# z of two images projected during the first scan, PE's pieces admitted by their weight, and DVE's readers of PE placed behind the product

## The chip, the core and the metric

The kernel runs on one core of a Trainium2 chip. A core has five engines, each of which takes its own instructions in order: PE (TensorE, matrix products and transposes into PSUM), DVE (VectorE), ACT (ScalarE), POOL (GpSimd) and SP (SyncE, which here issues nearly all DMAs). [...] The metric is the device time of one execution in microseconds (us); lower is better.

## What is computed

Four images of 384 channels and 48 x 48 pixels go through four layers, each of the form x + layer(group norm(x)). Cut to what matters here:

```
# layer 0, a selective scan over the 2304 pixels (D_INNER 768, D_STATE 16)
xz = xs @ in_proj_w.T;  xin, z = split(xz)            # z is what is moved
xin = silu(causal_conv4(xin) + conv_b)
dt, B, C = split(xin @ x_proj_w.T);  dt = softplus(dt @ dt_proj_w.T + dt_proj_b)
h[t] = exp(dt*A) * h[t-1] + dt*B[t]*x[t]              # per channel and state
y[t] = sum_s h[t]*C[t] + xin*D
out = layer_norm((y * silu(z)) @ out_proj_w.T)
# layer 1: 1x1 conv, 8x8 FFT filter, 3x3 depthwise conv, gelu gate, 1x1 conv
# layer 2: 11x11 depthwise conv with kernels built from 4 points
# layer 3: 4 experts (384 -> 384 -> 384), the two best of them weighted by a router
```

z depends on the input image alone: it needs the group norm's mean and deviation of x, and x. Nothing of the recurrence enters it.

## The kernel before

**Chunks and scans.** Layer 0 is worked in chunks of 460 (the last 464) pixels, five an image, twenty in all (`G`). A chunk has 96 scans, one for a block of 128 channels (6 blocks, taken in pairs) and one of 16 states. A scan is one DVE instruction over the 460 pixels. The main loop in `scans` (line 556 on) has one turn, or slot, for each of the 1920 scans; within it every engine's instructions are written out by hand in the order in which they are to stand (`tc.manual_schedule`).

In slot u: ACT makes the decay `da` a few scans ahead (L826), POOL makes the drive `bu` three scans ahead (L837), DVE scans (L850), and the state is multiplied with C, in "fast" slots by DVE at once (`product_now`, L870), in "slow" slots by POOL in the next slot (`product`, L879). A third of the slots are slow in image 0, a half afterwards. PE transposes each product and adds it into y (`turned`, L770). B and C arrive by DMA, spread over the partitions (`spread`, L814), some slots ahead.

**Everything else is tasks.** Each other part of the work is a generator that yields before every step the kind of step ("pe", "act", "dve", "pool"), a weight, the PSUM ring it needs room in, and a condition. A `Lane` (L92) holds a queue and a few active tasks. In each slot the lanes are asked twice: for ACT steps at the start, and after the scan for all others; each task makes at most one step per call. `wait(n)` is n empty steps.

There are three lanes. `aux` holds the rest of layer 0, planned by `plan` (L984) with a due slot for each task in a chunk: `project` (x of the next chunk), `project_z` (z of this one, L666 to L684), `gates` (silu), `expand`, `steps`, `gate` (y times z, L895), `out_proj`, `layer_norm`, `residual`, and for the next image `image_stats`, `image_norm` and `fold`, which scales a half of in_proj's weights by the image's deviation. `one` holds layers 1 to 3's router of the image before (`later`, L1127), `two` the experts of that image (`experts`, L1547). So image 0's scan has only `aux` beside it, the next three scans run beside the later layers of the image before, and after the last scan come what is left of the experts of image 2, and image 3's layers 1 to 3.

**The backlog.** `Meter` (L62) keeps an estimate of PE's backlog in us. Each slot drains 2.3 and adds 0.44 for the scan's transposes; a step of PE adds its weight. A lane other than `aux` may not start a weighted step while the value is over the limit:

```
if weight and self.bound and self.meter.value > self.meter.limit:
    continue
...
meter = Meter(2.3, 2.0)
```

**What DVE does between scan and product.** Steps of kind "dve" of all lanes stand after `scan(u)` and before `product_now(u)`. Many of them read a result of PE out of PSUM: an expert's output (`ye` L1641, `xe` L1644), layer 1's and 2's results (`uf` L1225, `xr` L1311, `xb` L1437), the gate (`zs` L907) and the experts' bias (`nb` L1587).

## Time and profile before

| | us |
|---|---|
| median of 3 runs | 5437.34 |
| lowest, highest | 5428.49, 5438.78 |
| the profiled execution | 5425.31 |
| its span, first to last instruction | 5423.4 |

The profile's page gives for the whole span PE 86% busy, DVE 75%, POOL 62%, ACT 55%. Those are averages over stages with different limits. The span in 40 slices of 136 us shows them (digits are tenths of busy time):

```profile
PE   5677677687678988988789999988899999999899
DVE  5999989889998788899887778899977674452200
POOL 3878878876678788765667678775777673000000
PEclk8788788788789999999899999999999999999899
```

Slices 1 to 7 are image 0's scan, up to slice 33 follow the other three, and the rest is the tail. A row of the windows, which the prediction uses, gives for a stretch "from:to length", then for each engine its busy time and, in brackets, its instructions; then PE's granted clock as a share of full speed, the mean busy share of the 16 DMA engines, and GB/s. A matmul of 32-bit numbers is two records. Busy times of PE are unions of overlapping records, so the mean length of one matmul in the groups is longer than what it costs in a row of many.

The products of z alone, by the windows restricted to their tile, for the scans of images 0, 1, 2 and 3 (PE, PE's weight loads, ACT, then clock and DMA of the stretch):

```profile
87.00:1016.50 929.50, 85.12 (x180) 36.01 (x180) 19.11 (x30) 0.81 0.47 136
1016.50:2128.30 1111.80, 81.22 (x180) 35.43 (x180) 19.01 (x30) 0.87 0.49 141
2128.30:3338.00 1209.70, 74.56 (x180) 31.70 (x180) 19.18 (x30) 0.95 0.56 162
3338.00:4525.00 1187.00, 75.91 (x180) 32.40 (x180) 19.14 (x30) 0.95 0.57 160
```

### The profile page before, as it was taken

To read this page: it belongs to the slowest core of one execution; us is meant where nothing else is said; L and a number is where in the kernel's file an instruction comes from. 1 tells how busy PE (TensorE), PEld (TensorE's weight loads), DVE (VectorE), ACT (ScalarE), POOL (GpSimd) and SP (SyncE) were. 2 spreads that over 40 slices of the span, in tenths; PEclk is the share of its full clock that TensorE was granted. 3 is DMA by queue.
4 is the path that set the end of the run, shared out by engine and by line. 5 is a ranking of instruction groups with operands and counts; after the bars stand their busy time and mean duration, and the time that the engine had idled before them with its cause. 6 is when DMAs were issued, how large, how long until landed. Compare 5 with 4: busy or idle time off the path is not lost. (4 is left out here: it accounts for less than half of the span.)

```text
span 5423.4 us, 81753 instructions
## 1 busy us (share of the span) xinstructions
PE 4666.9 (86%) x27796; PEld 3676.0 (68%) x27796; DVE 4053.8 (75%) x5581; ACT 2985.2 (55%) x6632; POOL 3365.2 (62%) x3020
## 2 busy tenths in 40 slices
PE   5677677687678988988789999988899999999899
PEld 4444454454347767665678887765678878889799
DVE  5999989889998788899887778899977674452200
ACT  3565565565558765655467655665566653334321
POOL 3878878876678788765667678775777673000000
PEclk8788788788789999999899999999999999999899
DMA  4445445454345555644566566554655554543200
GB/s 123 138 136 148 127 128 146 126 150 132 106 129 150 146 161 164 177 143 139 155 169 176 149 170 171 156 158 129 170 157 169 157 167 143 166 140 112 64 27 23
DMA packets 628391, 758.95 MB, mean 140 GB/s; under 512 B 58869, under 2 KB 622181, under 8 KB 627582
## 3 DMA queue, kind: packets, MB, share of 16 engines
q1 hardware_dynamic: 617668, 751.98, 48.2%
q8 instruction: 221, 3.62, 0.3%
q10 hardware_dynamic: 10298, 1.67, 0.2%
q14 instruction: 204, 1.67, 0.1%
HBM read 663.81 MB, written 89.65 MB: 139 GB/s over the span
## 5 line engine op out<-in xcount | busy, mean ns | idle before, releaser
L837 POOL TENSOR_TENSOR bu<-u,B 128x460 f32<-128x460 f32 (+1 forms) x1920 | 2227.5, 1170 | 778.2 <-DVE g L850 395.5
L826 ACT ACTIVATE da<-dt,a_neg 128x460 f32<-128x460 f32 (+1 forms) x1920 | 1242.8, 649 | 281.9 <-DVE g L870 185.4
L770 PE MATMUL y<-ident,g 128*115 128x128 f32 (+1 forms) x7680 | 1140.2, 297 | 274.1 <-DVE g L870 164.1
L770 PEld LDWEIGHTS y<-ident,g 128*115 128x115 f32 (+1 forms) x7680 | 1011.0, 187 | 502.3 <-DVE g L870 199.2
L879 POOL TENSOR_TENSOR g<-g,C 128x460 f32<-128x460 f32 (+1 forms) x885 | 1030.5, 1164 | 276.8 <-ACT carry L864 270.4
L850 DVE TENSOR_TENSOR_SCAN da<-da,carry,bu 128x460 f32<-128x460 f32 (+1 forms) x828 | 971.3, 1173 | 133.3 <-ACT da L826 94.7
L850 DVE TENSOR_TENSOR_SCAN g<-da,carry,bu 128x460 f32<-128x460 f32 (+1 forms) x708 | 819.7, 1167 | 83.5 <-ACT da L826 35.3
L870 DVE TENSOR_TENSOR g<-da,C 128x460 f32<-128x460 f32 (+1 forms) x1035 | 653.9, 632 | 91.7 <-PE y L770 31.5
L864 ACT COPY carry<-da 128x1 f32<-128x1 f32 x828 | 130.5, 158 | 824.3 <-DVE g L870 821.2
L1609 PE MATMUL pout<-hr,we 128*128 128x144 f32 x3456 | 483.6, 296 | 41.7 <-ACT hr L1625 31.7
L1609 PEld LDWEIGHTS pout<-hr,we 128*128 128x128 f32 x3456 | 455.4, 196 | 64.9 <-ACT hr L1625 42.6
L1609 PE MATMUL ph<-xe,we 128*128 128x144 f32 x3456 | 470.1, 291 | 13.4 <-DMA xe<-x3d 7.5
L1609 PEld LDWEIGHTS ph<-xe,we 128*128 128x128 f32 x3456 | 446.8, 194 | 30.6 <-issue 7.6
L1416 PE MATMUL pc<-band,row 128*128 128x162 f32 (+14 forms) x3456 | 458.8, 287 | 6.3 <-ACT row L1403 6.0
L1416 PEld LDWEIGHTS pc<-band,row 128*128 128x128 f32 x3456 | 446.2, 196 | 11.9 <-ACT row L1403 7.5
L1274 DVE SCALAR_TENSOR_TENSOR dw<-pad,w_dw,dw 128x384 f32<-128x384 f32 x576 | 347.6, 614 | 17.6 <-ACT pad L1249 6.7
L642 PE MATMUL pin<-xch,w_inx 128*128 128x463 f32 (+2 forms) x720 | 327.9, 595 | 34.7 <-DMA xch<-in_x 15.2
L921 PE MATMUL po<-w_out,zs 128*115 128x384 f32 (+1 forms) x960 | 341.5, 499 | 6.9 <-DVE dt L750 6.4
L1625 ACT ACTIVATE hr<-ph,nb 128x144 f32<-128x144 f32 x576 | 176.4, 377 | 305.2 <-PE ph L1609 303.6
L674 PE MATMUL pinz<-xch,w_inz 128*128 128x460 f32 (+1 forms) x720 | 316.8, 578 | 0.0
L1383 ACT ACTIVATE rep<-x,br,wr 128x192 f32<-128x192 f32 x576 | 274.3, 541 | 4.2 <-issue 4.2
L661 DVE SCALAR_TENSOR_TENSOR xc<-pin,conv_w,xc 128x460 f32<-128x460 f32 (+1 forms) x360 | 249.2, 692 | 30.9 <-ACT xc L655 19.2
(202 smaller groups left out, 5797.6 us busy)
## 6 DMA issues: line engine op xcount, KB each, us to landing
B<-bcd SPq DMA_DIRECT2D x768, 230.0 KB, 3.5
C<-bcd SPq DMA_DIRECT2D x768, 230.0 KB, 3.7
B<-bcd SPq DMA_DIRECT2D x192, 232.0 KB, 3.7
C<-bcd SPq DMA_DIRECT2D x192, 232.0 KB, 4.2
xe<-x3d SPq DMA_DIRECT2D x192, 216.0 KB, 2.8
ye<-y3d SPq DMA_DIRECT2D x144, 216.0 KB, 2.8
y3d<-ye SPq DMA_DIRECT2D x96, 216.0 KB, 2.2
xs<-x1d SPq DMA_DIRECT2D x24, 576.0 KB, 4.6
```

The source lines that it names most:

```text
L642: nc.tensor.matmul(ps[:, lo : halo + n], lhsT=w_inx[:, k, bass.ts(j, P)], rhs=c["x"][:, k, lo : halo + n], start=k == 0, stop=k == CT - 1,)
L674: nc.tensor.matmul(ps[:, :n], lhsT=w_inz[:, k, bass.ts(j, P)], rhs=c["x"][:, k, DCONV - 1 : DCONV - 1 + n], start=k == 0, stop=k == CT - 1,)
L770: nc.tensor.matmul(c["y", m][:w, bass.ts(k, P)], lhsT=src[:, bass.ts(k, w)], rhs=ident, is_transpose=True, start=c["terms", m] == 1 and k ...
L826: nc.scalar.activation(da[:, :n], c["dt", p][:, m % 2, :n], AF.Exp, scale=a_neg[:, m, s : s + 1])
L837: nc.gpsimd.tensor_mul(bu[:, :n], c["u", p][:, m % 2, :n], live["B", u // 2][:, :n])
L850: nc.vector.tensor_tensor_scan(here[:, :n], da[:, :n], bu[:, :n], last if t else nil[:, 0:1], ALU.mult, ALU.add,)
L870: nc.vector.tensor_mul(live["g", u][:, :n], live["h", u][:, :n], live["C", u // 2][:, :n])
L879: nc.gpsimd.tensor_mul(g[:, :n], g[:, :n], live["C", u // 2][:, :n])
L921: nc.tensor.matmul(ps[:w, :C], lhsT=c["zs"][:, m, bass.ts(k, w)], rhs=w_out0[:, m, :], start=m == 0, stop=m == MT - 1,)
L1274: nc.vector.scalar_tensor_tensor(v, src, w_dw[:, ct, k : k + 1], v, ALU.mult, ALU.add)
L1416: nc.tensor.matmul(d["acc2"][0][:, : BANDS[k] * W].rearrange("p (h w) -> p h w", w=W)[:, lo - edges[k] : hi - edges[k], xlo:xhi], lhsT=d[" ...
L1609: nc.tensor.matmul(ps[:, bass.ts(m, EB)], lhsT=w[:, k, bass.ts(m, P)], rhs=of[:, k, :], start=k == 0, stop=k == CT - 1,)
```

## The change

Three things are changed together.

*z of images 3 and 2 early.* A new lane `start` (width 4, bound by the meter) runs in image 0's scan, between `aux` and the other lanes. For images 3 and 2 it takes the statistics of x, normalises, folds z's half of in_proj, loads x chunk by chunk, makes z and stores it to DRAM (`zd`). In the scans of images 2 and 3 `project_z` fetches the chunk's z with one DMA into `zs`, and the statistics of x and the fold of z fall away there.

*The backlog.* The weight of the step itself counts, and the limit is 3.7 in place of 2.0.

*A third call of the lanes in each slot.* Kind "late" stands behind `product_now`. Steps of DVE that read a PSUM result of `gate`, `patches` (`uf`), `finish_strip` (`xr`), `windows` (`xb`), the experts' `begin` (`nb`) and `block` (`ye`, `xe`) become "late"; other DVE steps, also those that read PSUM in `project`, `steps` or `residual`, stay where they were. A task makes no two steps in one slot, whatever their kinds.

```diff
+PHASE = {"act": 0, "late": 2}
...
     def move(self, slot=0):
-        self.after = slot + 1 if self.next and self.next[0] == "act" else 0
+        self.after = slot + 1 if self.next else 0
...
-    def step(self, act, slot, at=0):
+    def step(self, phase, slot, at=0):
...
-            if (kind == "act") != act or task.after > slot:
+            if PHASE.get(kind, 1) != phase or task.after > slot:
                 continue
-            if weight and self.bound and self.meter.value > self.meter.limit:
+            if weight and self.bound and self.meter.value + weight > self.meter.limit:
                 continue
...
+            def early_stats(b, ct, h):
+                yield ("pool", 0, (early["xs"], 1))
+                t, k = early["xs"].take(f"xs0_{b}_{ct}_{h}")
+                half = HW // 2
+                nc.sync.dma_start(t, a["x"][b, bass.ts(ct, P), bass.ts(h, half)])
+                yield from wait(4)
+                st = early["stats", b]
+                for k3 in range(3):
+                    yield ("dve",)
+                    nc.vector.bn_stats(st[:, ct, h, k3, :], t[:, bass.ts(k3, LB)])
+                early["xs"].done(k)
...
+            def early_fold(b):
...
+                nc.sync.dma_start(w, per_channel(a["L0_in_proj_wT"])[:, :, DI:])
+                yield from wait(4)
+                for k in range(CT):
+                    yield ("act",)
+                    nc.scalar.activation(
+                        w[:, k, :], w[:, k, :], AF.Copy, scale=rstd0[:, b, k : k + 1]
+                    )
+                yield ("pe", 2.0, (ring, 1))
+                ps, r = ring.take(f"pbz{b}")
...
+            def early_load(b, t):
+                yield ("pool", 0, (early["x"], 1))
+                x, _ = early["x", b, t] = early["x"].take(f"xz{b}_{t}")
+                cols = bass.ds(starts[t], CHUNKS[t])
+                nc.sync.dma_start(x[:, :, : CHUNKS[t]], strip(a["x"][b], cols))
+                yield from wait(4)
+
+            def early_z(b, t, j):
+                n = CHUNKS[t]
+                x, xk = early["x", b, t]
+                yield ("pe", 2.3, (ring, 1), lambda: early["z"].free())
+                ps, r = ring.take(f"pz{b}_{t}_{j}")
+                z, zk = early["z"].take(f"z{b}_{t}_{j}")
+                for k in range(CT):
+                    nc.tensor.matmul(
+                        ps[:, :n],
+                        lhsT=early["w", b][:, k, bass.ts(j, P)],
+                        rhs=x[:, k, :n],
+                        start=k == 0,
+                        stop=k == CT - 1,
+                    )
...
+                yield ("act",)
+                nc.scalar.activation(
+                    z[:, :n], ps[:, :n], AF.Identity, bias=early["nz", b][:, j : j + 1]
+                )
+                ring.done(r)
+                yield ("pool",)
+                nc.sync.dma_start(zd[b][bass.ts(j, P), bass.ds(starts[t], n)], z[:, :n])
+                early["z"].done(zk)
...
             def project_z(i, j):
                 (b, t), c = G[i], st[i]
                 n, d = CHUNKS[t], batch[b]
+                if b in EARLY:
+                    if j == 0:
+                        c["zs"] = wk.tile([P, MT, TM], F32, name=f"zs{b}_{t}", tag="zs", bufs=1)
+                        nc.sync.dma_start(
+                            c["zs"][:, :, :n],
+                            zd[b].rearrange("(m p) t -> p m t", p=P)[:, :, bass.ds(starts[t], n)],
+                        )
+                    yield from wait(5)
+                    return
                 yield ("pe", 2.3, (ring, 1))
...
-                yield ("dve",)
+                yield ("late",)
                 zm = c["zs"][:, m, :n]
                 nc.vector.tensor_tensor(zm, ps[:, :n], zm, ALU.mult)
...
+            EARLY = (3, 2)
+            zd = {b: dram.tile([DI, HW], F32, name=f"zd{b}") for b in EARLY}
...
+            start = Lane(4, meter)
+            start.queue += early_tasks()
...
                 for u in range(N + 6):
+                    if u == LEN * NC:
+                        start.drain(u)
+                        first_image.close()
...
-                    for lane in (aux, *lanes):
-                        lane.step(False, u)
+                    for lane in (aux, start, *lanes):
+                        lane.step(1, u)
                     if u < N:
                         product_now(u)
+                    for lane in (aux, start, *lanes):
+                        lane.step(2, u)
...
-        meter = Meter(2.3, 2.0)
+        meter = Meter(2.3, 3.7)
```

## The prediction

> **What bounds the kernel now.** Three views, read in this order. First the windows of the run by stage: preparation, the scans of images 0, 1, 2 and 3 (cut where scan 0, 480, 960, 1440 starts), and the tail behind the last scan.
>
> ```profile
> core 0: us, PE busy (x) PEld busy (x) DVE busy (x) ACT busy (x) POOL busy (x), PEclk, DMA share, GB/s
> 87.00:1016.50 929.50, 665.55 (x2960) 450.83 (x2960) 845.37 (x1036) 536.44 (x1122) 772.15 (x686) 0.81 0.47 136
> 1016.50:2128.30 1111.80, 912.03 (x4779) 656.81 (x4780) 972.06 (x1291) 683.24 (x1469) 861.68 (x773) 0.87 0.49 141
> 2128.30:3338.00 1209.70, 1096.69 (x6757) 868.11 (x6756) 997.51 (x1360) 733.80 (x1641) 863.06 (x772) 0.95 0.56 162
> 3338.00:4525.00 1187.00, 1087.83 (x6813) 878.00 (x6812) 977.81 (x1321) 720.91 (x1633) 860.39 (x769) 0.95 0.57 160
> 4525.00:5423.40 898.40, 857.43 (x6343) 791.92 (x6341) 233.15 (x515) 287.19 (x736) 4.59 (x15) 0.97 0.31 90
> ```
>
> Image 0's scan is DVE's (845 of 930 us) and leaves PE 264 us idle; in those of images 2 and 3 PE is busy 91% and DVE 82%; the tail is PE's (95%). So the same PE microsecond is cheap in the first stage and dear in the last three.
>
> Second, the same windows by chunk (96 scans). These are the first, fourth and fifth chunks of images 1 and 2, in that order:
>
> ```profile
> 1016.50:1220.10 203.60, 161.22 (x742) 106.19 (x742) 181.17 (x236) 124.56 (x276) 173.44 (x159) 0.87 0.51 145
> 1706.10:1928.70 222.60, 208.06 (x1358) 172.09 (x1356) 176.37 (x223) 168.42 (x390) 172.85 (x155) 0.94 0.51 147
> 1928.70:2128.30 199.60, 178.22 (x1041) 131.51 (x1041) 176.00 (x229) 113.08 (x190) 173.09 (x154) 0.93 0.57 167
> ...
> 2128.30:2358.10 229.80, 211.08 (x1278) 165.17 (x1277) 189.49 (x271) 136.22 (x320) 173.59 (x159) 0.97 0.58 169
> ...
> 2876.40:3117.10 240.70, 231.89 (x1604) 200.15 (x1603) 179.30 (x229) 169.94 (x402) 172.31 (x154) 0.97 0.56 161
> 3117.10:3338.00 220.90, 209.60 (x1328) 165.17 (x1328) 175.16 (x228) 130.29 (x235) 171.49 (x152) 0.95 0.62 174
> ```
>
> Chunks at one place of two images do the same work for layer 0, but image 2's carry more expert products. They price a PE microsecond: first place +49.9 us of PE and +26.2 of time, 0.52; fourth +23.8 and +18.1, 0.76; fifth +31.4 and +21.3, 0.68. The second place gives 0.14 (192 to 227 of PE, 262 to 267 of time; DVE is busy 240 and 247 there), the third 0.61. No place gives 1.
>
> Third, what DVE waits for in image 2's scan:
>
> ```profile
> DVE ye L1641 <- PE pout L1609: 43.1, 29, 3.9
> DVE da L850 <- ACT carry L864: 21.3, 6, 6.8
> DVE da L850 <- ACT da L826: 21.1, 28, 2.2
> DVE g L850 <- ACT da L826: 13.7, 17, 1.6
> DVE g L870 <- PE y L770: 11.6, 13, 1.9
> ```
>
> The columns are us in total, times, longest. The worst single wait is DVE standing at a result of the experts on PE, with the product and the next scan queued behind it. In image 3's scan that row is 39.7 us.
>
> [...] 0.81 granted in the first stage, 0.95 at 91% busy; so a fuller first stage should get some of its added work back in clock. [...] The trace shows the cost for 1152 KB: w_inx lands in 6.5 us and w_inz in 8.3, against 3.5 for B.
>
> **The change, part by part.** I counted the instructions that stand between one scan and the next in the emitted orders of both kernels.
>
> *z leaves images 2 and 3.* 36 PE records a chunk go (18 products, two passes each). The windows restricted to pinz give 74.6 us for 180 in image 2's scan and 75.9 in image 3's, so 14.9 a chunk. The lanes refill a part: experts gain 54 products in image 2 (108 records by 0.14 us, +15) and lose 27 in image 3 (-7.6). With a fold of w_inz less in image 2, PE's work changes by place: image 2 -19.8, -15.7, -0.4, -2.5, -25.9; image 3 -15.3, -12.3, +1.2, -14.0, -38.0 (in the last, no expert work is left to let in). Times the slopes: image 2 -10, -2, 0, -2, -18 = -32; image 3 -8, -2, +1, -11, -26 = -46. ACT loses 30 zs activations an image by 0.64 us; it is 61% busy, so nothing.
>
> *Statistics leave images 1 and 2.* 18 bn_stats by 0.53 us and a normalisation each, about 10 us of DVE an image; stage 1 is DVE's (972 of 1112). I take half: -5 and -5.
>
> *The tail.* The experts stand earlier: about 102 products (204 records by 0.12 us, from x36 in 4.41 us in the chain of waits) are done before the last scan and not after it: -25. PE is saturated there, so in full.
>
> *What image 0's scan gets.* 180 products: pinz takes 85.1 us for 180 records there, so 360 cost 170; two folds (pbz) some 12. They stand between scans 57 and 290; none is left for the drain at scan 480. DVE gets 36 bn_stats (19.2) and two normalisations (6), all in the first chunk; ACT 60 activations by 0.64 and two folds (44). First chunk: DVE rises from 164 to 189; image 1's first chunk with DVE 181 takes 203.6, so 178.5 becomes about 203: +25. Second and third chunk: PE rises from 130 to about 199 at the old clock, 178 at 0.93; the chunk above with PE 178, DVE 176 takes 199.6, though its POOL is busier (173 against 154): 185 and 188 become about 197 each, +21. Fourth +4. Sum +50. DVE hides PE's rise; if the clock stays at 0.81 PE becomes the bound, the slower rival below.
>
> *z is fetched.* One DMA of 1380 KB a chunk, 10 in all, on SP's queue before the B and C loads. B is issued some four scans (9 us) before POOL needs it. POOL waits for B 14.0 us in 8 times in image 2's scan now. Lower end 0 (hidden as most are), upper end 4 us each, 40; I take +8. Its own reader, the silu some 30 scans later, does not wait. Besides, SP waits there for out_proj to have read zs, but the task starts only after DVE has handled that result; nothing. In image 0, 60 stores, 10 x loads and 12 statistics loads bring about 30 MB to 126; the DMA share was 0.47: nothing.
>
> *DVE's readers of PE behind the product.* The order within a scan becomes scan, product, reader, where it was scan, reader, product. In half of the scans (the fast ones) there is a product, 0.63 us, so PE gets that much more before DVE stands at it. Waits of the moved kinds (ye, xe, xb, zs, xr, nb) are 67 us in image 2, 66 in image 3, 15 in image 1, 13 in image 0, some 120 waits over the page's threshold. At most 0.63 in half of them is 38 us, plus ACT's next decay, which no longer waits behind them. The PSUM bank is free up to 0.63 us later, a loss if PE were short of banks; I see no such wait near the head of its list. From +15 to -50; I take -20.
>
> *The backlog.* A piece was let in at a value up to 2.0, whatever its weight, so up to 4.3 stood; now weight included it may reach 3.7. The drain stays at 2.3 a slot, so throughput stays, with a lower peak. -20 to +15; I take -3.
>
> Sum: +50 -5 -32 -5 -46 -25 +8 -20 -3 = -78. The profiled execution took 5425.3 us (span 5423.4), the median shown is 12 us above it; the difference carries over: 5437 - 78, about **5360 us**.
>
> **Rivals.**
> - *B, PE's work converts in full* (5290). If PE is really the bound in the chunks where it leads, the cuts in the first, fourth and fifth places count whole, -115; tail -25, image 1 -10, image 0 +35 thanks to the clock, readers -30: -145. For it: 91% busy, and DVE waiting for PE. Against: the measured slopes below 1, and POOL at 173 us in every chunk.
> - *C, another engine takes the place* (5430). POOL and DVE, coupled by B, C, carry and PSUM, hold the slots as they do at the first place, and only the last chunks gain: -25, tail -25, image 0 +60, fetch +8, readers -20: about -5. For it: the second and third places hardly react.
> - *D, slower: PE becomes the bound of image 0's scan* (5475). At the old clock, scans 57 to 290 need 1.37 + 0.73 us of PE each; at the 91% filling of later stages 2.3 us, against 1.93 now: +87, and +25 of DVE before. The later stages then give -50 and the tail -25. It decides once image 0's scan takes over 1030 us. For it: these products are admitted at 2.3 a slot while slots there are shorter. Against: the clock's rise, and products only every fourth scan.
>
> That the change does not do what it says is excluded: ten fetches, five an image, stand in place of the 180 products.
>
> **How the numbers follow.** Forecast 0.50 (own range 5315 to 5405), B 0.22, C 0.15, D 0.13. Range 5285 to 5440: it takes in B's centre and C, and leaves out D and B's far end. About 0.2%, 11 us, is what a measurement of this kernel can tell from no change. Within it falls a part of C, 0.07; faster 0.78 (the forecast, B, C's better part); slower 0.15.
>
> **What would show it.** The scan of image 0 at about 980 us with clock near 0.9; images 2 and 3 near 1160 and 1130, the gain in the first, fourth and fifth chunks; the tail near 873; ye's wait halved; POOL's wait for B under 25 us an image. It is wrong if image 0 passes 1030, or if image 3's last chunk stays above 205.

## The result and the profile after

| | before | after |
|---|---|---|
| median, us | 5428.57 | 5409.83 |
| lowest, highest | 5416.32, 5438.78 | 5405.14, 5416.61 |
| the profiled execution | 5425.31 | 5405.14 |

The ratio is 0.9963, with a 95% interval of 0.9949 to 0.9977: the change makes the kernel 0.37% faster, about 20 us, where 78 were forecast. The direction is right and the size is a quarter of it. (The medians are of seven executions each; the three of the kernel before that are given further up are among them.)

The windows by stage of the kernel after, as they were shown of before (scans of images 0, 1, 2, 3, then the tail):

```profile
86.50:1046.60 960.10, 773.38 (x3440) 508.84 (x3440) 867.71 (x1091) 572.39 (x1188) 775.18 (x688) 0.87 0.55 163
1046.60:2160.60 1114.00, 913.47 (x4882) 657.67 (x4882) 964.14 (x1274) 686.45 (x1481) 860.67 (x773) 0.89 0.47 138
2160.60:3344.20 1183.60, 1045.51 (x6636) 852.48 (x6636) 993.62 (x1340) 718.83 (x1617) 861.21 (x772) 0.94 0.58 168
3344.20:4516.40 1172.20, 1031.10 (x6569) 846.15 (x6567) 985.91 (x1318) 706.02 (x1597) 858.62 (x768) 0.93 0.59 168
4516.40:5403.10 886.70, 835.87 (x6122) 771.40 (x6122) 227.80 (x498) 281.71 (x717) 4.25 (x14) 0.96 0.31 89
```

The first stage costs 30.5 us more (929.6 to 960.1), image 1 2.2 more; image 2 gives 26.1, image 3 14.8, the tail 11.7. Image 1 was to become about 5 us shorter and did not. The other stages move the way that was forecast, but the three that gain give about half of it or less. For images 2 and 3 together the prediction's marks (1160 and 1130 us) meant 107 us, and 41 came.

By chunk: the second and third chunk of image 0, where most of the products of z now stand, first before and then after, and the first, fourth and fifth of image 2 after.

```profile
265.40:450.20 184.80, 129.98 (x588) 86.67 (x588) 170.61 (x212) 109.89 (x244) 153.80 (x138) 0.84 0.46 137
450.20:638.10 187.90, 133.25 (x588) 88.95 (x588) 170.68 (x211) 110.01 (x244) 154.17 (x138) 0.82 0.47 135
...
284.40:479.00 194.60, 174.06 (x765) 112.47 (x766) 171.35 (x212) 124.73 (x270) 154.56 (x138) 0.92 0.60 179
479.00:669.70 190.70, 171.71 (x737) 107.28 (x735) 171.74 (x211) 122.71 (x269) 154.71 (x138) 0.94 0.60 179
...
2160.60:2379.70 219.10, 191.70 (x1187) 155.74 (x1188) 185.05 (x255) 130.72 (x307) 173.14 (x159) 0.96 0.62 181
...
2886.40:3124.60 238.20, 226.86 (x1661) 200.87 (x1660) 185.15 (x233) 170.09 (x403) 172.54 (x154) 0.98 0.58 170
3124.60:3344.20 219.60, 193.77 (x1236) 155.20 (x1234) 173.24 (x231) 114.05 (x209) 171.57 (x153) 0.95 0.61 178
```

In image 0 the granted clock rises from 0.84 and 0.82 to 0.92 and 0.94. PE's busy time rises by 82 us in the two chunks, and the chunks grow by 13: most of it is hidden. In image 2's last chunk PE is busy 194 us where it was 210, DVE and POOL as before, and the chunk takes 219.6 where it took 220.9: 16 us of PE are gone, and 1 us of time.

What DVE waits for in image 2's scan, and POOL's row for B in the same stretch (`g` L986 is the product, L966 the scan):

```profile
DVE da L966 <- ACT da L942: 34.2, 24, 6.1
DVE g L986 <- DMA C<-bcd: 21.8, 11, 5.8
DVE g L986 <- PE y L886: 19.3, 16, 3.5
DVE ye L1782 <- PE pout L1750: 11.9, 8, 2.5
DVE xb L1578 <- PE pc L1557: 10.1, 7, 2.2
```

```profile
POOL bu L953 <- DMA B<-bcd: 53.7, 22, 7.2
```

The wait of `ye` that stood first is down from 43.1 to 11.9 us. That looks like the work of the late readers, but it is not: the same kernel with its readers in front of the product (`e_nolate`, below) shows

```profile
DVE ye L1782 <- PE pout L1750: 11.0, 18, 1.8
```

in the same image. Meanwhile `g`, the product that now stands ahead of the readers, waits 19.3 for PE (11.6 before) and 21.8 for C (0.8 before), and POOL's wait for B is 53.7 (14.0 before). So other waits have grown while this one fell.

### The profile page after: what moved, and what is told of

Read it like the earlier page. It is cut to its first block, busy times and chain, and to the rows that moved or that the text cites. A ratio compares the mean times of both kernels' runs of the same rounds, so it can differ in the third digit from the quotient of the medians.

```text
span 5403.1 us, 82006 instructions
## 1 busy us (share of the span) xinstructions
PE 4646.1 (86%) x27796; PEld 3666.7 (68%) x27796; DVE 4067.1 (75%) x5581; ACT 2989.0 (55%) x6632; POOL 3363.1 (62%) x3020
## 5 line engine op out<-in xcount | busy, mean ns | idle before, releaser
L886 PE MATMUL y<-ident,g 128*115 128x128 f32 (+1 forms) x7680 | 1111.3, 292 | 192.5 <-DVE g L986 114.8
L886 PEld LDWEIGHTS y<-ident,g 128*115 128x115 f32 (+1 forms) x7680 | 991.2, 183 | 400.4 <-DVE g L986 140.5
L966 DVE TENSOR_TENSOR_SCAN da<-da,carry,bu 128x460 f32<-128x460 f32 (+1 forms) x828 | 971.7, 1174 | 122.2 <-ACT da L942 76.7
L966 DVE TENSOR_TENSOR_SCAN g<-da,carry,bu 128x460 f32<-128x460 f32 (+1 forms) x708 | 819.8, 1167 | 57.7 <-issue 18.8
L986 DVE TENSOR_TENSOR g<-da,C 128x460 f32<-128x460 f32 (+1 forms) x1035 | 656.4, 634 | 175.7 <-DMA C<-bcd 62.0
L1750 PE MATMUL ph<-xe,we 128*128 128x144 f32 x3456 | 484.7, 298 | 33.6 <-DMA xe<-x3d 18.9
L1750 PEld LDWEIGHTS ph<-xe,we 128*128 128x128 f32 x3456 | 459.4, 199 | 51.5 <-DMA xe<-x3d 13.7
L1557 PEld LDWEIGHTS pc<-band,row 128*128 128x128 f32 x3456 | 440.0, 194 | 16.6 <-ACT row L1544 11.9
L749 PE MATMUL pin<-xch,w_inx 128*128 128x463 f32 (+2 forms) x720 | 344.8, 621 | 55.1 <-DMA xch<-in_x 32.3
L1524 ACT ACTIVATE rep<-x,br,wr 128x192 f32<-128x192 f32 x576 | 273.7, 540 | 4.2 <-issue 4.2
L749 PEld LDWEIGHTS pin<-xch,w_inx 128*128 128x128 f32 x720 | 143.8, 213 | 179.8 <-issue 136.3
```

The source lines that it names most:

```text
L749: nc.tensor.matmul(ps[:, lo : halo + n], lhsT=w_inx[:, k, bass.ts(j, P)], rhs=c["x"][:, k, lo : halo + n], start=k == 0, stop=k == CT - 1,)
L886: nc.tensor.matmul(c["y", m][:w, bass.ts(k, P)], lhsT=src[:, bass.ts(k, w)], rhs=ident, is_transpose=True, start=c["terms", m] == 1 and k ...
L966: nc.vector.tensor_tensor_scan(here[:, :n], da[:, :n], bu[:, :n], last if t else nil[:, 0:1], ALU.mult, ALU.add,)
L986: nc.vector.tensor_mul(live["g", u][:, :n], live["h", u][:, :n], live["C", u // 2][:, :n])
L1524: nc.scalar.activation(rep[:, :, n, :, :].rearrange("p g r c -> p r g c"), rows.rearrange("p (r g c) -> p r g c", r=BR, c=BC), AF.Identity ...
L1557: nc.tensor.matmul(d["acc2"][0][:, : BANDS[k] * W].rearrange("p (h w) -> p h w", w=W)[:, lo - edges[k] : hi - edges[k], xlo:xhi], lhsT=d[" ...
```

## The experiments

In all of them the ratio is to the kernel before, each with its 95% interval. "Early z" is the first of the three changes, "new admission" the second (the changed rule of the backlog), "late readers" the third. The stages come from one profiled execution each. Such an execution can lie some 10 us from the median of its kernel (`e_prodfirst` 5433.7 against 5423.1, `e_early_14` 5446.6 against 5455.6), so a smaller difference between the stages of two kernels says little by itself.

"Experts left" counts in the program's order the matrix products behind the last scan. In every kernel it is, here and in the expectations, 1350 higher than the products of images 0 to 2's experts alone: of these 1141 are left before and 1039 in the changed kernel (the trace of the kernel before has 2286 PE records of L1609 behind the last scan, two a product). Only the differences between rows are used.

| early z | new admission | late readers | label | ratio | interval | image 0 | images 1 to 3 | tail | experts left |
|---|---|---|---|---|---|---|---|---|---|
| | | | before | 1 | | 929.6 | 3508.5 | 898.4 | 2491 |
| x | | | e_earlyonly | 1.0039 | 1.0025 to 1.0053 | 960.0 | 3511.2 | 881.8 | 2383 |
| | x | | e_meteronly | 1.0022 | 1.0013 to 1.0031 | 930.6 | 3507.7 | 911.4 | 2554 |
| | | x | e_lateonly | 1.0066 | 1.0049 to 1.0083 | 929.7 | 3528.1 | 920.5 | 2502 |
| x | x | | e_nolate | 0.9916 | 0.9900 to 0.9932 | 967.1 | 3462.4 | 860.1 | 2311 |
| x | | x | e_oldmeter | 0.9980 | 0.9973 to 0.9987 | 964.7 | 3480.5 | 882.0 | 2375 |
| | x | x | e_noearly | 1.0059 | 1.0044 to 1.0073 | 929.9 | 3494.7 | 936.7 | 2637 |
| x | x | x | after | 0.9963 | 0.9949 to 0.9977 | 960.1 | 3469.8 | 886.7 | 2389 |

| label | ratio | interval | image 0 | images 1 to 3 | tail | experts left |
|---|---|---|---|---|---|---|
| e_z_held | 0.9947 | 0.9931 to 0.9962 | 929.1 | 3485.2 | 901.4 | 2491 |
| e_z_freed | 0.9943 | 0.9926 to 0.9959 | 929.5 | 3500.5 | 876.9 | 2383 |
| e_z_held_meter | 1.0004 | 0.9993 to 1.0015 | 930.0 | 3491.0 | 914.7 | 2554 |
| e_six | 0.9951 | 0.9935 to 0.9966 | 963.5 | 3460.3 | 885.2 | 2389 |
| e_nolate_six | 0.9910 | 0.9893 to 0.9927 | 964.1 | 3459.4 | 858.9 | 2311 |
| e_prodfirst | 0.9991 | 0.9981 to 1.0001 | 969.7 | 3514.5 | 860.0 | 2313 |
| e_late_again | 1.0044 | 1.0028 to 1.0060 | 980.3 | 3542.8 | 839.8 | 2187 |
| e_nolate_33 | 0.9919 | 0.9901 to 0.9938 | 956.9 | 3439.4 | 912.5 | 2566 |
| e_nolate_41 | 1.0029 | 1.0018 to 1.0039 | 960.2 | 3550.0 | 841.0 | 2246 |
| e_early_14 | 1.0047 | 1.0031 to 1.0064 | 960.8 | 3495.4 | 901.6 | 2502 |

### One part undone

The first theory, F, was read from POOL's 53.7 us: the fetch of z makes B and C late and eats the gain. Its rivals were that the engines' coupling holds the slots (S), and that the late readers are to blame (R). A bank is here one of the PSUM buffers in the kernel's rings (beside the scans three in `mm` and one in `acc`); the planner lets a step of PE that writes into a ring start only when one of them is free. `e_noearly` takes early z out of the changed kernel:

```diff
-            EARLY = (3, 2)
+            EARLY = ()
```

> The changed kernel with no image's z made early (statistics, folds and products of z as in the kernel before); the late readers and the new admission stay. Theory F (the fetch of z delays the B and C loads and eats what the moved products bring): the readers and the admission bring their 20 to 25 us by themselves, so 0.995 to 0.996 of before, as fast as the changed kernel, and POOL's wait for B in the scans of images 2 and 3 is back near 30 us (it is 106 in the changed kernel). Rival S (the slots are held by the coupling of DVE, POOL and ACT, so neither part converts): within 0.2% of before. Rival R (the late readers themselves make B and C late, since DVE and POOL reach them sooner): B's wait stays near 100 us without any fetch.

Measured 1.0059. Without early z the other two parts do not bring 20 us, they cost 32. No theory had that. Images 1 to 3 are 14 us shorter, but 2637 expert products are left, 146 more than before, and the tail is 38 us longer. POOL waits for B 20 us in image 2 and 44 in image 3 though nothing is fetched, so the fetch is not the only source of that wait. (The 106 us of the expectation are all of POOL's waits for DMAs in images 2 and 3 of the changed kernel; those for B are 53.7 and 36.7.)

`e_nolate` puts the readers back:

```diff
-                yield ("late",)
+                yield ("dve",)
```

(in all six places)

> The changed kernel with the six late readers of DVE back in front of the product. By the prediction's term the time rises by 20 us over the changed kernel (about 0.9995 of before), DVE's wait for PE results rising by about 40 us in the scans of images 2 and 3. Theory F: B's wait on POOL there stays near 106 us. Rival R: it falls to 30 to 50 us and the time rises by less than 10 us.

Measured 0.9916, 26 us below the changed kernel (0.0047 of 5428), where 20 above were predicted. POOL's wait for B stays (47 us in image 2, 45 in image 3), so R does not hold as it was put: the readers do not cause that wait, and the wait is there in the faster kernel. Here is the tail of this kernel, to be held against the last of the five rows of the changed kernel above:

```profile
4516.30:5376.30 860.00, 814.21 (x5973) 748.53 (x5971) 224.68 (x485) 278.44 (x703) 4.25 (x14) 0.97 0.30 89
```

149 PE records fewer stand in the tail and it is 26.7 us shorter; images 1 to 3 differ by 7 us. So beside the other two parts the late readers cost their time mostly in the tail: 78 products of the experts that `e_nolate` lets in before the last scan are left behind it.

`e_oldmeter` has the old rule:

```diff
-            if weight and self.bound and self.meter.value + weight > self.meter.limit:
+            if weight and self.bound and self.meter.value > self.meter.limit:
...
-        meter = Meter(2.3, 3.7)
+        meter = Meter(2.3, 2.0)
```

> The changed kernel with the admission of before (value over 2.0, weight not counted). By the prediction's term +3 us over the changed kernel, within plus or minus 10. If the admission shapes the DMA traffic (expert pieces in bursts), B's wait changes by over 20 us and the time with it, either way.

Measured 0.9980, 9 us slower than the changed kernel, within what was expected. POOL's wait for B falls to 26 and 23 us, and the kernel does not become faster: a second sign that this wait is cheap, though the order of the program changed as well.

`e_six` fetches z in portions:

```diff
-                    if j == 0:
-                        c["zs"] = wk.tile([P, MT, TM], F32, name=f"zs{b}_{t}", tag="zs", bufs=1)
-                        nc.sync.dma_start(
-                            c["zs"][:, :, :n],
-                            zd[b].rearrange("(m p) t -> p m t", p=P)[:, :, bass.ds(starts[t], n)],
-                        )
+                    yield ("pool",)
+                    if "zs" not in c:
+                        c["zs"] = wk.tile([P, MT, TM], F32, name=f"zs{b}_{t}", tag="zs", bufs=1)
+                    nc.sync.dma_start(
+                        c["zs"][:, j, :n], zd[b][bass.ts(j, P), bass.ds(starts[t], n)]
+                    )
                     yield from wait(5)
```

> The changed kernel with a chunk's z fetched in six DMAs of 230 KB, four scans apart, in place of one of 1380 KB: the same bytes in portions as large as a B load. Theory F with the burst as cause: POOL's wait for B in images 2 and 3 falls from 106 to 40 to 60 us, DVE's for C from 52 to 20, the time by 20 to 35 us (about 0.991 of before). Rival S: waits move, the time stays within 8 us. Rival R: B's wait stays over 90 us.

Measured 0.9951, 0.0012 or 7 us under the changed kernel; the two intervals overlap. Over images 2 and 3 POOL's wait for B goes from 90 to 83 us and the product's wait for C from 52 to 46, where F asked for 40 to 60 and 20. F as the main cause has fallen.

### One part alone

`e_earlyonly` is `e_nolate` with `e_oldmeter`'s edit on top.

> The kernel before with z of images 3 and 2 made early, and nothing else: old admission, readers in front of the product. The prediction's terms for this part add up to -55 us. If the parts add, it is the changed kernel's 19 us gain plus what the late readers cost (30) less what the admission brings (6): about -43, 0.992 of before, with 2383 expert products in the tail. If admission and early z need each other, it is over 0.994.

Measured 1.0039, 21 us slower than before. The prediction gave this part -55. The first stage costs 30 and the tail gives 17, but images 1 to 3 take 3511 us, as before, although 180 products of z have left them and only 108 of the experts have come. Against this kernel `e_oldmeter` (0.9980) has the late readers in addition, and there they gain: 0.0059, or 32 us, 31 of them in images 1 to 3.

`e_meteronly` has the new rule in the kernel before:

> The kernel before with the new admission alone (weight counted, limit 3.7). 2554 expert products are left for the tail against 2491, so the tail is 15 to 18 us longer. If the admission shortens the scans by itself, as it does with early z (3511 to 3462 us for images 1 to 3), -50 and +17: about 0.994. If it needs the room that early z leaves, the scans stay within 15 us: 1.000 to 1.003.

Measured 1.0022, the second of the two answers: scans unchanged, tail longer.

`e_lateonly` is `e_noearly` with `e_oldmeter`'s edit:

> The kernel before with the six late readers alone (old admission, no early z). 2502 expert products are left for the tail against 2491: same tail within 5 us. If the late readers bring by themselves what they bring with early z under the old admission (5450 to 5416), -33: 0.994. If they bring something only there: within 0.2% of before. Slower by 20 or more would say that they harm by themselves.

Measured 1.0066, the third answer: the late readers harm by themselves, 20 us in images 1 to 3 and 22 in the tail. The groups of DVE over the whole run follow; the last numbers of a row are the idle time before the group and what ended it. Before:

```profile
L870 DVE TENSOR_TENSOR g<-da,C 128x460 f32<-128x460 f32 (+1 forms) x1035 | 653.9, 632 | 91.7 <-PE y L770 31.5 <-DMA C<-bcd 9.9 <-DVE da L850 0.5
L1641 DVE TENSOR_TENSOR ye<-pout,ye 128x432 f32<-128x432 f32 x144 | 87.0, 604 | 168.6 <-PE pout L1609 145.1 <-DMA xe<-x3d 9.2 <-DMA ye<-y3d 4.8
```

With the late readers alone:

```profile
L986 DVE TENSOR_TENSOR g<-da,C 128x460 f32<-128x460 f32 (+1 forms) x1035 | 656.4, 634 | 144.2 <-PE y L886 62.4 <-DMA C<-bcd 20.0 <-issue 0.7
L1782 DVE TENSOR_TENSOR ye<-pout,ye 128x432 f32<-128x432 f32 x144 | 86.9, 604 | 166.5 <-PE pout L1750 138.9 <-DMA ye<-y3d 14.0 <-DMA xe<-x3d 10.8
```

The product, which now follows the scan at once, stands idle 52 us more, 31 of it at `PE y`: it writes into one of six buffers `g`, and PE has yet to transpose what an earlier product left there. The reader's 168.6 and 166.5 hide a shift, since they include the tail, where no product stands. The waits of image 2's scan show it, to be held against the rows of the prediction (43.1 and 11.6):

```profile
DVE ye L1782 <- PE pout L1750: 29.9, 21, 3.4
DVE g L986 <- PE y L886: 27.6, 19, 5.7
```

In images 2 and 3 together `ye` waits 60.0 us where it waited 82.8, and the product waits 48.9 for `PE y` where it waited 20.5; all of DVE's waits there are 392 us where they were 385. DVE now comes to PE earlier, at the product, and is held up there instead. In the tail, 11 more products explain 2 or 3 of the 22 us, at the 0.2 us each by which `e_nolate_33` and `e_nolate` differ there; the rest stays open.

### What a PE microsecond in the scans is worth

The forecast stood on slopes of 0.14 to 0.76, four of the five above 0.5. `e_z_held` measures the price by itself: in the kernel before, the products of z of images 2 and 3 are left out, and every other instruction stays in its place. (The ACT step reads x in place of PE's result, so its wait for PE goes too.)

```diff
+                skip = b >= 2
-                for k in range(CT):
+                for k in range(1 if skip else CT):
+                    w = 1 if skip else n
                     nc.tensor.matmul(
-                        ps[:, :n],
+                        ps[:, :w],
...
                 nc.scalar.activation(
-                    c["zs"][:, j, :n], ps[:, :n], AF.Identity,
+                    c["zs"][:, j, :n],
+                    c["x"][:, j % CT, DCONV - 1 : DCONV - 1 + n] if skip else ps[:, :n],
+                    AF.Identity,
```

> The kernel before without the matrix products that make z in images 2 and 3: two of three products of each block are left out and the third has one column; zs is written by the same ACT step from x instead, so z of these images is not computed. PSUM banks, the backlog's weights and so the place of every other instruction stay. 180 products, some 149 us of PE, are gone and nothing comes in their stead. Prediction's slopes (0.52, 0.14, 0.61, 0.76, 0.68 of a PE microsecond by place): 14.9 us a chunk give -81 us, about 5346, 0.985 of before. Rival P (a PE microsecond in a scan is nearly free, the slopes came from the DVE and ACT work that expert products bring along; a fit over the chunks of ten profiles gives 0.04 us for a product of z): -5 to -20 us, over 0.996.

Measured 0.9947 (0.9931 to 0.9962), -20 to -37 us, where the slopes gave -81 and rival P -5 to -20. Its windows for the scans of images 2 and 3:

```profile
2130.50:3332.10 1201.60, 1054.75 (x6634) 857.87 (x6635) 997.09 (x1360) 734.29 (x1641) 862.10 (x772) 0.93 0.57 162
3332.10:4500.50 1168.40, 1040.67 (x6696) 863.13 (x6695) 979.90 (x1321) 722.55 (x1633) 859.41 (x769) 0.93 0.57 162
```

and the first and fifth chunk of image 2, and the fourth and fifth of image 3 (the last two before, which were not shown yet, stand at the end):

```profile
2130.50:2361.80 231.30, 202.09 (x1251) 163.60 (x1252) 190.07 (x270) 135.87 (x320) 173.40 (x159) 0.94 0.58 166
...
3117.30:3332.10 214.80, 200.89 (x1304) 162.14 (x1303) 174.76 (x228) 130.48 (x235) 171.14 (x152) 0.93 0.62 179
...
4060.40:4295.40 235.00, 219.68 (x1599) 194.80 (x1598) 178.55 (x220) 169.38 (x405) 172.50 (x153) 0.99 0.58 166
4295.40:4500.50 205.10, 192.04 (x1405) 169.69 (x1404) 166.66 (x209) 118.72 (x226) 167.40 (x149) 0.95 0.66 190
...
4060.10:4309.40 249.30, 240.34 (x1622) 206.06 (x1621) 179.18 (x220) 168.76 (x405) 172.88 (x153) 0.95 0.57 160
4309.40:4525.00 215.60, 206.16 (x1426) 176.12 (x1425) 164.27 (x209) 118.09 (x227) 167.77 (x149) 0.95 0.63 179
```

Two things are to be read there. First, the scans of images 2 and 3 shrink from 2396.7 to 2370.0 us: 27 us for 149 of PE, 0.18 (0.14 to 0.25 by the interval of the ratio). The first chunk of image 2, with PE busy 92% before, does not react at all (229.8 to 231.3); only three of the ten chunks give over 5 us (220.9 to 214.8, 249.3 to 235.0, 215.6 to 205.1). What is gained comes from the fourth and fifth chunks of both images, in which PE was busy 95 or 96% of the time: these four give 33 us, and the other six lose 6. Second, PE's busy time falls by 89 us and not by 149 (2184.5 to 2095.4). Of the 60 us between, the other matmuls take 41: the union of their 13208 records grows from 2051.6 to 2092.6 us as the granted clock goes from 0.95 to 0.93. The rest is mostly overlap of z's records with their neighbours'. So a PE that is busy 91% of these two stretches did not set their length.

`e_z_freed` leaves the same work out and gives its bank and its weight free as well:

```diff
+                if b >= 2:
+                    yield ("act",)
+                    if "zs" not in c:
+                        c["zs"] = wk.tile([P, MT, TM], F32, name=f"zs{b}_{t}", tag="zs", bufs=1)
+                    nc.scalar.activation(
+                        c["zs"][:, j, :n], c["x"][:, j % CT, DCONV - 1 : DCONV - 1 + n],
+                        AF.Identity, bias=d["nwm", 1][:, j : j + 1],
+                    )
+                    return
```

> The same work left out (z of images 2 and 3 is not computed, zs is written by ACT from x), but with neither bank nor weight held, so that expert products may come in: 2383 are left for the tail, as in the kernel with early z alone, 2491 before. No first-stage work and no fetch. Prediction: scans -55, tail -25, so 0.985. Rival P: tail -17 to -26 and the scans within 15 us, so about 0.996. Against the kernel with early z alone, whose scans of images 1 to 3 take 3511 us: what these scans are shorter here is the price of the fetch (theory F: 30 to 50 us; otherwise under 15).

Measured 0.9943, near rival P's answer. The scans of images 1 to 3 are 8 us shorter than before and the tail 21.5. Against `e_z_held` these scans are 15 us longer: that is what the 108 expert products that moved in cost there. By the prediction's 0.14 us a record they are 30 us of PE, so their price is about 0.5 of a PE microsecond, an estimate from two single executions. The slopes were near the truth for expert work, which brings steps of ACT and DVE with it, and not for PE's time alone.

Against `e_earlyonly`, with the same 2383 products left, images 1 to 3 are 11 us shorter here: 8 us longer in image 1, and 18 shorter in images 2 and 3, where the fetch stands. The kernels differ also in where the statistics and folds are made, so this bounds the fetch only roughly; theory F's 30 to 50 us are not there.

`e_z_held_meter` is `e_z_held` under the new rule:

> The kernel before with the new admission, and without the products that make z in images 2 and 3 (one column of one product in three is left, zs is written from x, so z is not computed there); every other instruction stands as with the new admission alone (5440 us). Theory A (with a tighter backlog a PE microsecond converts, with the old one it does not): -60 to -80, 5360 to 5380. Theory P (it is nearly free under both): -15 to -30 as under the old admission, 5410 to 5425.

Measured 1.0004, 10 us below `e_meteronly`, where 29 came under the old rule: theory A falls. The new admission does not raise the price of a PE microsecond.

### Late readers without the late bank

A bank that a late reader frees can be filled only in the next slot. Theory K made this the cause of the readers' cost. `e_prodfirst` has the readers as "dve" again and moves the product itself, which puts all other DVE steps of the lanes behind it too:

```diff
+                    if u < N:
+                        product_now(u)
                     for lane in (aux, start, *lanes):
                         lane.step(1, u)
-                    if u < N:
-                        product_now(u)
```

> The changed kernel with the six readers back in the common call of the lanes, and the product itself moved ahead of that call: DVE still meets every reader of PE behind the product, but a PSUM bank is free for pieces of PE in the same call again. 2313 products of image 0 to 2's experts stand behind the last scan, as with the readers in front (2311), against 2389 in the changed kernel. Theory K (the late readers cost because a bank comes free one call later, so fewer expert products are let in before the last scan, and the tail pays for them): 5360 to 5382 us, tail near 860. Rival H (a reader behind the product is itself harmful, since PE, ACT or POOL get its result or bank later): 5400 us or more.

The tail is 860.0 us, as with the readers in front, so K is right on the tail. Its sum is not: 0.9991, since images 1 to 3 take 3514.5 us, 52 more than `e_nolate` (this execution was 11 us above its median). The sum is the one H gave. But here all other DVE steps stand behind the product too, and the changed kernel, with the six readers there alone, is only 7 us above `e_nolate` in these scans. So the product at once behind the scan is no gain, and how much of the 52 us is the readers' is not shown.

`e_late_again` fills the bank in the same slot:

```diff
-                    for lane in (aux, start, *lanes):
-                        lane.step(2, u)
+                    for phase in (2, 1):
+                        for lane in (aux, start, *lanes):
+                            lane.step(phase, u)
```

> The changed kernel with one more call of the lanes behind the late readers, so that a bank freed there can be filled in the same slot. 2187 expert products are left for the tail, 202 fewer than in the changed kernel. Theory K: the tail falls by 45 to 50 us, the scans of images 1 to 3 take the 57 us of PE at 0.5 to 0.7 each, so 5385 to 5400 in all. Rival H: tail shorter, but scans longer by as much or more, 5405 to 5420.

The tail is 839.8 us, 47 less than in the changed kernel, as K says. Images 1 to 3 are 73 us longer, more than either theory expected, and the ratio is 1.0044. Both halves of the trade are real, and letting in more is not the cure.

### The limit of the backlog

Early z and the new rule are each slower alone and 0.84% faster together. Three neighbours of the pair:

```diff
-        meter = Meter(2.3, 3.7)
+        meter = Meter(2.3, 4.1)
```

> Early z and the new admission, readers in front, with a limit of 4.1 in place of 3.7. 2246 expert products are left for the tail against 2311, which takes 16 us off it. Ordered effect of the backlog: the scans of images 1 to 3 lie between 3462 (limit 3.7) and 3511 us (old admission), so 5370 to 5400 in all. Scatter: outside of that.

Measured 1.0029; the scans take 3550 us, above the range given, which was to be the mark of scatter.

> The same with a limit of 3.3. 2566 products are left for the tail, 255 more, which add 60 us to it. Ordered effect: the scans fall below 3455 us, and the sum is 5410 to 5440, since the tail loses more than the scans gain. Scatter: scans above 3462.

Measured 0.9919, below the range: the scans take 3439 us and the tail 912.5 (an execution 8 us above the median).

`e_early_14` has the old rule with `Meter(2.3, 1.4)`:

> Early z, readers in front, and the old rule (weight not counted) with the limit lowered to 1.4, so that a piece of 2.3 reaches the same 3.7, while small pieces are held back too. 2502 products are left for the tail, 191 more than with the new admission, which add 47 us. If the peak of the backlog is what shortens the scans, they take 3450 to 3475 us and the sum is 5410 to 5435; if not, scans near 3511 and 5470.

Measured 1.0047; the scans take 3495 us, between the two answers. Under the new rule the scans grow with the limit (3439, 3462, 3550 for 3.3, 3.7, 4.1) and the tail falls (912.5, 860.1, 841.0). In sum 3.3 and 3.7 cannot be told apart and 4.1 is 61 us slower; no lower limit was run. The old rule with the same peak for a large piece is not on this line, so the peak alone does not settle it.

`e_nolate_six`, the version that the first group pointed to:

> The changed kernel with the six readers in front of the product and a chunk's z fetched in six DMAs of 230 KB. If both gains add (30 and 13 us), 5366 us, 0.989 of before; if the six DMAs only helped where the late readers stood, 5379, 0.9915.

Measured 0.9910, the best of all; the six DMAs add nothing that can be told from `e_nolate`. Either beats both kernels: the change without its late readers.

## Why the prediction was wrong

The step that failed first is the price of a PE microsecond in the scans of images 2 and 3: the prediction took the work of z there at slopes of 0.14 to 0.76, 0.54 in the mean (-81 us for 149), and left out with all else in place it is worth 0.18 (-27 us). The second is the sign of the late readers: -20 was forecast, +26 was measured. And the prediction added the parts, which the eight kernels of the first table do not allow. Here is what each part does to the time, in us, by the differences of their ratios (each to within some 10 us):

| part | predicted | alone | beside one other | beside both others |
|---|---|---|---|---|
| early z | -55 | +21 | -58 (new admission), -47 (late readers) | -52 |
| new admission | -3 | +12 | -67 (early z), -4 (late readers) | -9 |
| late readers | -20 | +36 | -32 (early z), +20 (new admission) | +26 |

By its own steps:

- **z leaves images 2 and 3, times the slopes: wrong, and the largest error.** The slopes compared chunks of images 1 and 2 that differ in more than PE: in the first place, by the prediction's own lines, DVE's busy time rises by 8 us and ACT's by 12 beside PE's 50. Taken alone, PE's 149 us are worth 27, not 81. That early z brings -52 us in the changed kernel, where its terms add up to -55, is luck: it comes as +30 in image 0, -25 in images 1 to 3 and -50 in the tail, because 248 more expert products are done before the last scan (`e_noearly` against the changed kernel). The remark that no expert work was left to let in in image 3's last chunk does not hold either: 510 PE records of the experts start there before and 645 after.
- **PE busy 91% as the sign of a dear microsecond.** It is 91 and 92% in the scans of images 2 and 3, where 149 us of PE left out made 27 us of time, and 95% in the tail, where 43 us of PE less made 38 us (`e_nolate` against the kernel before). The union of the weight loads' records fills 72% and 74% of the scans of images 2 and 3 before (868.1 of 1209.7, 878.0 of 1187.0) and 88% of the tail (791.9 of 898.4), so it sets the tail further apart. By the sum of the records, which overlap in this trace, the shares are 104, 107 and 134%. No run here shows what price goes with which share.
- **DVE's readers behind the product: wrong in sign.** The bounds were +15 to -50; +26 was measured beside the other two parts, +36 and +20 in two other settings, and -32 in one, beside early z under the old admission. The remark that a bank comes free 0.63 us later looked for a wait of PE in the profile. One cost is elsewhere: in the program's order a piece that finds no free bank waits for the next slot, so fewer expert products precede the last scan (`e_prodfirst` fills the bank in the same slot and has the shorter tail). The other is that the product itself waits for PE where the reader did. That the wait of `ye` was more than halved, as forecast, is luck too: the new admission alone brings it to 23.3 us in image 2, and with early z, readers in front, it is 11.0. Why the readers gain in the one setting is not shown.
- **The backlog, -3: no single number.** It is -9 beside the other two parts, +12 alone, and -67 beside early z without the late readers.
- **What image 0's scan gets: right in kind, 50 predicted, 30.5 measured.** The clock rose, as the prediction expected: 0.81 to 0.87 over the stage. The first chunk grew by 19 us where 25 were forecast; the second and third together grew by 13 where 21 were. Rival D did not come near (it needed 1030 us; the stage took 960).
- **The tail, -25: -12.** The count of products was right (102). PE's busy time in the tail falls by 22 us, and a part of that is lost at one change of experts, where PE waits for the scaled weights (the trace of the changed kernel, waits of PE in the tail):

```profile
PE pb L1719 <- ACT we L1712: 7.2, 1, 7.2
```

- **The fetch, +8: not contradicted, and not measured apart** (11 us over images 1 to 3, 18 in images 2 and 3 alone, by two single profiles). The sign set for it failed: POOL's wait for B was to stay under 25 us an image and was 54 and 37. But this wait is no price of the fetch: it is 20 and 44 us in `e_noearly`, where nothing is fetched. That it would make the B and C loads behind it late was an estimate: the landing times that the prediction quotes (6.5 and 8.3 us for 1152 KB, 3.5 for B) show how long a large load takes, and over images 2 and 3 B's 230 KB landed in a median 3.7 us before and 3.8 after, C's in 4.0 and 4.3.
- **Statistics, -10: not seen.** DVE's busy time in image 1 falls by 8 us, and the stage does not get shorter.

Neither of the two signs of being wrong came true: image 0 stayed under 1030 us, and image 3's last chunk came to 201.9. They watched steps other than the two that failed. Of the rivals, C (another engine takes the place, -5) came nearest in kind, and the measured time lies between it and the forecast. `e_z_held` agrees with it in that the chunks at the end of an image gain; that POOL and DVE hold the slots is argued, as no run makes them faster. B, PE's work converts in full, is refuted by `e_z_held`.

Open remains why early z and the new admission need each other. Under the new rule z's products left out with their place held give 10 us, while taking their bank, their weight and their slots out as well (`e_nolate` against `e_meteronly`) lets 243 more expert products in and shortens images 1 to 3 by 45 us. That points at the place of z's pieces in the planner, which `aux` starts whatever the backlog is, and not at their PE time; no run here isolates it (`e_z_freed` under the new rule would). Chunks also move against their work: the second chunks of images 2 and 3 take 7 and 9 us more in the changed kernel than before (267.1 to 273.7, 263.0 to 272.1), with 4 us of PE less in one and 1 more in the other. So a part of the pair's size may be the order that happened to come out.

## What to carry to other kernels

That PE was busy 91% of two stages did not make its time dear (0.18 us came for each one left out): before counting on freed PE time, leave the work out with everything else held in place, and see what the stage gives. Where a planner decides by banks and a backlog what comes in, each edit changes what is admitted and what is left for the tail, so look at both sums, and test the parts of a change alone and in pairs. Moving a consumer behind other work of its engine may only move the wait, where that other work waits for the same producer: with the late readers alone `ye` waited 23 us less in images 2 and 3 and the product 28 us more for PE. Here the move made the kernel slower in three settings of four (by 36, 20 and 26 us, and 32 faster in the fourth).

## What the runs showed of the hardware

With 149 us of its work left out in two stages, PE's busy time fell by only 89: the granted clock went down from 0.95 to 0.93 in both, and the other matmuls took 41 us longer. In the second and third chunk of image 0 it went up, from 0.84 and 0.82 to 0.92 and 0.94, when work was added; over that stage the added work, 182 us by the durations that the prediction used, raised PE's busy time by 108. So in these stages the clock went with the load, and PE time removed came out smaller (89 for 149), and PE time added cheaper (108 for 182), than a count by durations says.

On DVE a waiting reader held up what was written behind it: in image 2's scan of the kernel before, DVE stood idle for 2.53 us at one `ye`, until PE's `pout` was there (2507.80 to 2510.33), and the product of the scan that had ended at 2507.80 started behind that reader, at 2510.86.
